# Clears moved beside an expert layer, an opening put in order of use, and three tiles' weights fetched during an attention

## The chip, the core and the metric

The kernel runs on one core of a Trainium2 chip. The metric is the device time in microseconds (us) of one execution; it is shown as the median of a few executions. TensorE (PE) multiplies, VectorE (DVE) and ScalarE (ACT) do elementwise work and reductions, GpSimd (POOL) does elementwise work and starts the gathers and scatters that go by an index, and SyncE (SP) starts most of the plain transfers. Each of these has its own queue of instructions and works through it in order.

## The reference, cut to what matters

Everything is float32. x has 4 batches of 512 rows of 256, and the context has 4 batches of 1601 rows of 256.

```
x = x + L0_xattn(ctx, layernorm(x))   # 8 heads of 128; keys and values from [layernorm(ctx), layernorm(latents)]
x = x + L0_ffn(layernorm(x))          # 8 experts 256->1024->256, top 2, at most 512 rows per expert
x = x + L1_xattn(ctx, layernorm(x))   # 8 heads of 32, keys and values from ctx
x = x + L1_ffn(layernorm(x))          # 8 experts 256->1024->256, top 2, no limit of rows
```

In L0_xattn the latents are normalized again with their own gamma and beta, and the queries attend to 1601 + 512 = 2113 rows.

## The kernel before

The kernel has four stages, one for each line above; they are called A, B, C and D here. A scheduler orders each engine's queue from the program text, except where `in_order` or `keep_in_program_order` fixes it. Buffers come from pools; a load into a buffer waits until the last reader of what lay there is done.

**Opening of A.** SP loads x of batch 0, small vectors, the whole context of batch 0, then `wq`, `wkv`, `wo`, and x of the other batches. DVE takes the moments of all 13 context tiles, then normalizes latents and context. PE turns them (`group`), and `kvin` is written with the columns in an interleaved order: column block b, quarter k, 32 columns. The 512 latents are the first columns of quarter 0. Only when all of `kvin` stands do `queries` and `keys` of head 0 start (L670, L685). PE also works out the product of the values' bias with `wo` (`ps_bo`, L802) here, and POOL adds the output bias to x (L601).

**The clears.** `clear_rows` writes zeros and a mark into two tables in device memory, `rows_a` (2048 rows of 265 numbers) and `rows_b` (18688 rows): 41 transfers on SP, 40 of 530 KB and one of half that, from a zero tile that holds four rows for each partition, so that 4,240 bytes in a row are written. `clear_slots` writes 4 MB of zeros to `slot_x` in 8 transfers, started by POOL. Both stand after the opening and ahead of the first attention step.

**Steps of A.** There are 128 steps n (batch, head, quarter of the queries). A step does `scores` (PE), the maximum `top` (DVE), the exponential `attn` (ACT), `exchange` (16 transfers that swap blocks of 32 partitions, 12 started by SP and 4 by ACT), and in the next step `turn` (DVE) gives `pT`. `weigh` (PE, `ps_o`) follows in steps n + 1 to n + 3. The scores have a single buffer, so the scores of step n + 1 wait for the exponential of step n. The lists `later[n]` put keys of the next head, values, the next batch's context (`load_ctx`, `keys_input`) and the routing of stage B between the pieces.

**B.** Keys and values of L1_xattn for two batches, from `cT`, then 8 experts; SP fetches each expert's weights (2 MB), its rows `sx`, and stores `slot_y`.

**C.** 16 units of 13 steps, with the order of PE, DVE, ACT and POOL written out by hand (`in_order`, L1342). `load_first_weights` (L1279) fetches the first half (1 MB) of expert 0's weights for stage D, in eight pieces of 128 KB, at the start of the last batch.

**D.** Tiles of 256 rows: 8 first tiles, one for each expert, then 13 further tiles and, if there are more, others. `first_tile` loads rows from `rows_a` and weights `w_e` (2 MB) from a pool of four buffers; `further_tile` gathers both by index. For each tile `turned` transposes the rows (PE, L1439), `hidden` is the first product (L1451), and `second` the second (L1470). `told` reads target rows and shares from the rows (DVE, L1401, L1429). During the first tiles `route2` and `table` route the last batch.

## Time and profile before

| | us |
|---|---|
| median of 3 runs (2989.96 to 2995.00) | 2993.43 |
| the profiled execution, its own time | 2993.88 |
| its span, first to last instruction | 2992.2 |

| stretch of the span | PE busy | granted clock | share of DMA |
|---|---|---|---|
| 0 to 45 (opening of A) | 13.84 | 1.00 | 0.75 |
| 45 to 145 (first steps of A) | 70.59 | 0.86 | 0.81 |
| 145 to 1640 (rest of A) | 1480.13 | 1.00 | 0.39 |
| 1640 to 1940 (B) | 284.13 | 0.97 | 0.31 |
| 1940 to 2645 (C) | 613.88 | 0.93 | 0.11 |
| 2645 to 2730 (first tiles of D) | 67.35 | 0.88 | 0.55 |
| 2730 to 2992 (rest of D) | 248.09 | 0.98 | 0.51 |

Each row is one stretch. PE busy is in us and is to be held against the length of the stretch; the clock is the share of full speed that PE was granted; the share of DMA is the mean busy share of the core's 16 DMA engines. In the lists of instructions that follow, a line gives start, duration, engine, line of the code, operation, output and input, and count; a bracket gives the idle time before it and what ended it.

### The profile page before, as it was taken

What the parts mean: (1) busy time and instruction counts of PE and PEld (TensorE: products, weight loads), DVE (VectorE), ACT (ScalarE), POOL (GpSimd) and SP (SyncE); (2) the same over time, 40 slices, a digit from 0 to 9 for tenths busy, and PEclk for the clock granted to TensorE, in tenths of its full rate; (3) what the DMA queues carried; (4) which work ended last, traced back from release to release, by engine and by line L of the source; (5) the groups of instructions that cost most, each with busy time, mean ns of one, the idle gap of its engine ahead of it and who ended that gap; (6) DMA issues with size and microseconds to landing.
All of it is one profiled execution on the core that took longest, in us unless ns stands there. A gap on an engine that the chain in (4) does not pass through costs nothing.

```text
span 2992.2 us, 35534 instructions
## 1 busy us (share of the span) xinstructions
PE 2778.0 (93%) x13426; PEld 1839.3 (61%) x13426; DVE 1456.4 (49%) x2324; ACT 933.3 (31%) x1312; POOL 400.0 (13%) x308
## 2 busy tenths in 40 slices
PE   5699999999999999999997999879989898898998
PEld 2466676667766667666665566634444444466887
DVE  4256447544475444554454200178777768741110
ACT  2133234323343233333331221124434344341221
POOL 1000000100001000000000100022314223333442
PEclk9899999999999999999998899979999999898999
DMA  8743334433344333333334333110101110055552
GB/s 297 236 124 95 98 92 103 117 92 89 95 113 109 90 94 91 99 93 97 95 94 120 117 106 115 47 46 17 28 24 41 29 37 23 11 181 169 185 173 72
DMA packets 165103, 295.95 MB, mean 99 GB/s; under 512 B 43287, under 2 KB 81752, under 8 KB 161848
## 3 DMA queue, kind: packets, MB, share of 16 engines
q1 hardware_dynamic: 124024, 204.45, 24.4%
q0 software_dynamic: 16320, 53.42, 5.9%
q10 hardware_dynamic: 24576, 35.68, 4.6%
q8 instruction: 109, 1.79, 0.3%
q14 instruction: 74, 0.61, 0.1%
HBM read 97.86 MB, written 49.76 MB: 49 GB/s over the span
## 4 chain that ended last, share of the span: by engine, by line
PE 82%; DVE 7%; issue 3%; DMA 3%; ACT 3%; SPq 2%; POOL 1%; POOLq 0%; DVEq 0%; ACTq 0%
PE ps_o L772 15%; PE ps_s L735 15%; PE ps_v L718 7%; PE ps_k L685 7%; PE ps_w L1188 6%; PE ps_y L1470 4%; PE ps_h L1451 4%; PE ps_h L970 4%; PE ps_y L983 4%; DVE tops L1149 2%; PE ps_o L1219 2%; DVE sum L1210 2%; PE ps_p L783 2%; PE ps_v L945 2%; PE ps_q L670 2%
## 5 line engine op out<-in xcount | busy, mean ns | idle before, releaser
L743 DVE TENSOR_REDUCE top<-ps_s 128x1 f32<-128x2113 f32 x128 | 301.8, 2358 | 574.8 <-PE ps_s L735 574.8
L772 PE MATMUL ps_o<-pT,v 128*128 128x256 f32 x2176 | 521.5, 382 | 7.7 <-DVE pT L764 7.7
L735 PE MATMUL ps_s<-kT,qT 128*128 128x512 f32 (+1 forms) x1280 | 488.9, 527 | 26.3 <-ACT attn L749 26.0
L772 PEld LDWEIGHTS ps_o<-pT,v 128*128 128x128 f32 x2176 | 411.4, 191 | 124.8 <-issue 70.3
L735 PEld LDWEIGHTS ps_s<-kT,qT 128*128 128x128 f32 x1280 | 241.8, 191 | 275.7 <-issue 239.9
L749 ACT ACTIVATE attn<-ps_s,top 128x2113 f32<-128x2113 f32 x128 | 259.0, 2024 | 486.5 <-DVE top L743 448.8
L764 DVE STREAM_TRANSPOSE pT<-swapped 128x2176 f32<-128x2176 f32 x128 | 312.4, 2441 | 70.8 <-DMA swapped<-attn 60.3
L1149 DVE TENSOR_REDUCE tops<-ps_s 128x2 f32<-128x1024 f32 (+1 forms) x224 | 237.4, 1104 | 135.2 <-PE ps_s L1138 135.0
L685 PE MATMUL ps_k<-kvin,wkv 128*128 128x512 f32 (+1 forms) x640 | 262.0, 534 | 5.0 <-ACT kT L692 5.0
L1188 PE MATMUL ps_w<-asked,keyed 64*128 64x256 f32 (+1 forms) x1664 | 244.2, 415 | 20.5 <-DVE tops L1149 9.5
L718 PE MATMUL ps_v<-wkv,kvin 128*128 128x256 f32 x1088 | 253.5, 381 | 0.0
L1201 ACT ACTIVATE pT<-ps_w 128x1024 f32<-128x1024 f32 (+1 forms) x176 | 179.5, 1024 | 192.5 <-PE ps_w L1188 190.4
L1188 PEld LDWEIGHTS ps_w<-asked,keyed 64*128 64x128 f32 (+1 forms) x1664 | 147.0, 189 | 143.2 <-ACT pT L1201 60.7
L718 PEld LDWEIGHTS ps_v<-wkv,kvin 128*128 128x128 f32 x1088 | 204.9, 190 | 32.7 <-issue 3.3
L1210 DVE TENSOR_TENSOR sum<-sum,pT 128x1024 f32<-128x1024 f32 (+1 forms) x128 | 181.0, 1414 | 10.7 <-ACT pT L1201 3.9
L692 ACT ACTIVATE kT<-ps_k,bqk 128x512 f32<-128x512 f32 (+1 forms) x160 | 97.3, 621 | 268.7 <-DMA swapped<-attn 129.8
L1210 POOL TENSOR_TENSOR sum<-sum,pT 128x1024 f32<-128x1024 f32 x48 | 124.1, 2585 | 345.7 <-ACT pT L1201 345.5
L685 PEld LDWEIGHTS ps_k<-kvin,wkv 128*128 128x128 f32 x640 | 116.5, 192 | 80.9 <-issue 67.1
L1451 PE MATMUL ps_h<-xT,w_e 128*128 128x256 f32 x640 | 143.9, 383 | 10.2 <-issue 10.2
L1138 PE MATMUL ps_s<-kT,qT 32*128 32x512 f32 (+1 forms) x1024 | 140.5, 577 | 12.5 <-ACT kT L936 6.8
L725 ACT COPY v<-ps_v 128x512 f32<-128x512 f32 x144 | 80.0, 561 | 224.9 <-PE ps_v L718 156.2
L1470 PE MATMUL ps_y<-w_e,hT 128*128 128x256 f32 x640 | 144.4, 385 | 0.0
(261 smaller groups left out, 2615.1 us busy)
## 6 DMA issues: line engine op xcount, KB each, us to landing
swapped<-attn SPq DMA_DIRECT2D x1536, 68.0 KB
swapped<-attn ACTq DMA_DIRECT2D x512, 68.0 KB
rows_b<-empty SPq DMA_DIRECT2D x36, 530.0 KB
w<-in_w_dram SPq DMA_DIRECT2D x16, 1024.0 KB
w_e<-in_wall_dram SPq DMA_DIRECT2D x7, 2052.0 KB
cT<-in_ctxT_dram SPq DMA_DIRECT2D x4, 1601.0 KB
keyed<-kT SPq DMA_DIRECT2D x32, 200.1 KB
ctx_b<-in_ctx_dram SPq DMA_DIRECT2D x4, 1536.0 KB
```

Source lines behind the costliest of these rows:

```text
L685: nc.tensor.matmul(ps[:, :n], lhsT=wkv[:, c, hs], rhs=flat_kvin[c][:, j0 : j0 + n], start=c == 0, stop=c == DC - 1,)
L718: nc.tensor.matmul(ps[:, k, :], lhsT=flat_kvin[c][:, j * P : (j + 1) * P], rhs=wkv[:, c, cols], start=c == 0, stop=c == DC - 1,)
L735: nc.tensor.matmul(flat[:, j0 : j0 + n], lhsT=qT[:, t * P : (t + 1) * P], rhs=kT[:, j0 : j0 + n], start=True, stop=True,)
L743: nc.vector.tensor_reduce(top, flat[:, :L], AX.X, ALU.max, negate=True)
L749: nc.scalar.activation(attn[:, :L], flat[:, :L], AF.Exp, bias=top, accum_out=total)
L764: nc.vector.transpose(pT[:, :, k * P : (k + 1) * P].rearrange("p c (a i) -> p a c i", a=4), swapped.rearrange("p a (c i) -> p a c i", i=32),)
L772: nc.tensor.matmul(ps, lhsT=v[:, j - parts[part][0], (h % 2) * DH0 : (h % 2 + 1) * DH0], rhs=pT[:, j, :], start=j == 0, stop=j == NB - 1,)
L1149: nc.vector.tensor_reduce(tops[u][:, t : t + at // n, 2 * pair : 2 * pair + 2, j0 // 512], of, AX.X, ALU.max,)
L1188: nc.tensor.matmul(ps[:r, s, pair * QH : (pair + 1) * QH], lhsT=keyed[o][64 * s : 64 * s + 64, pair, j * P : j * P + r], rhs=asked[u % 3][ ...
L1210: (nc.gpsimd if k else nc.vector).tensor_tensor(to, to, pT[:r], ALU.add)
L1451: nc.tensor.matmul(ps[:, f, :], lhsT=w(at, P), rhs=xT[:, c, :], start=c == 0, stop=c == DC - 1,)
L1470: nc.tensor.matmul(ps, lhsT=hT[:, f, r * P : (r + 1) * P], rhs=w(WB1 + f * D, D), start=f == 0, stop=f == FC - 1,)
```

## The change

1. `clear_rows` becomes a generator. It is advanced six transfers at a time in the expert loop of B, after the fetch of the next expert's weights. Its source is one row, read four times by a zero stride, so pieces are 1,060 bytes.
2. `clear_slots` is started by SP, one transfer at steps 4, 6, ... 18 of A.
3. The opening loads in order of use: first x and four context tiles, then the latents' vectors, head 0's slices of `wq` and `wkv`, then the rest. The moments go by groups of four tiles, and normalization moves from DVE to ACT. `keys` is cut by quarters, so that `keys(0)` needs the latents alone. The engines' order is fixed.
4. `ps_bo` and the output bias of batch 0 go to step 13 of A.
5. `load_first_weights` fetches the weights of three tiles (6 MB) into memory that C no longer uses; `room(k)` rotates D's weights through four places. The last, conditional tile shares these, where it had a place of its own.
6. Three tiles of integers come from a short-lived pool `brief`; the vectors of A reuse its memory. `counts_i` is made three tiles ahead of the end.

```diff
-    def clear_slots(zeros):
-        for i in range(SLOTS // (4 * P)):
-            nc.gpsimd.dma_start(
-                slot_x[i * 4 * P : (i + 1) * 4 * P, :].rearrange("(p r) d -> p r d", p=P), zeros
+    def clear_slots(zeros, i):
+        tc.keep_in_program_order(
+            nc.sync.dma_start(
+                slot_x[i * 4 * P : (i + 1) * 4 * P, :].rearrange("(p r) d -> p r d", p=P),
+                zeros.unsqueeze(1).to_broadcast([P, 4, D]),
...
+    brief = brief_of.enter_context(tc.tile_pool(name="brief", bufs=1))
+    iota_i = brief.tile([P, NT, E], I32, name="iota_i")
...
-                nc.sync.dma_start(
-                    some.rearrange("(p r) d -> p r d", p=P), empty[:, : some.shape[0] // P, :]
-                )
+                tc.keep_in_program_order(
+                    nc.sync.dma_start(
+                        some.rearrange("(p r) d -> p r d", p=P),
+                        empty.unsqueeze(1).to_broadcast([P, some.shape[0] // P, PAY]),
+                    )
+                )
+                yield
...
+        for n0 in range(0, NM - 1, 4):
+            nc.sync.dma_start(ctx_b[:, n0 : n0 + 4, :], of_ctx[:, n0 : n0 + 4, :])
+            if n0 == 0:
+                load_vectors(gbl, "gamma_lat", "beta_lat")
+                load_vectors(bqk, "bq", "bk", "bv")
+                nc.sync.dma_start(wq[:, :, :DH0], of_wq[:, :, :DH0])
+                nc.sync.dma_start(wkv[:, :, :DH0], of_wkv[:, :, :DH0])
+                load_vectors(gbm, "gamma_media", "beta_media")
...
-            def keys(j0):
-                n = min(512, LP - j0)
+            def keys(k):
+                n = 512 if k < 4 else P
...
-                        rhs=flat_kvin[c][:, j0 : j0 + n],
+                        rhs=kvin[:, c, : NB - 1, k, :] if k < 4 else kvin[:, c, NB - 1, :, :],
...
-        early, late = keys_input(0, ctx_b)
-        for s in early + late:
+        stats, turns = context[::2], context[1::2]
+        for s in (
+            latent[:2] + stats[:1] + latent[2:] + fill[:2] + stats[1:2] + turns[:1] + stats[2:3]
+            + turns[1:2] + fill[2:3] + stats[3:] + turns[2:3] + fill[3:4] + turns[3:] + fill[4:]
+        ):
             s()
-        empty = one.tile([P, 4, PAY], F32, tag="lat", name="empty")
-        clear_rows(empty)
-        clear_slots(empty[:, :, :D])
...
+        for i in range(SLOTS // (4 * P)):
+            later[4 + 2 * i].append(lambda i=i: clear_slots(empty, i))
+        later[13].append(output_bias)
...
             if e + 1 < E:
                 w_next = expert_weights(wexp, "w1", "w2", e + 1)
+                for _ in range(6):
+                    next(clear, None)
...
+            t = kv1.tile([P, KV], F32, tag="kv", name="w_kv")
+            rest = t[:, WIDE:]
+            nc.sync.dma_start(rest[:, : WIDE - WB1], a["wall"][:P, WB1:])
+            nc.sync.dma_start(t[:, :WIDE], a["wall"][P : 2 * P, :])
+            nc.sync.dma_start(cw[:, :WIDE], a["wall"][2 * P : 3 * P, :])
...
+        def room(k):
+            if k % 4 == 2:
+                return cw[:, :WIDE]
+            if k % 4 == 3:
+                return new.tile([P, WIDE], F32, tag="w", name="w_e")
+            return kv1.tile([P, KV], F32, tag="kv", name="w_e")[:, :WIDE]
...
-        more.append(lambda: further_tile(SURE, spare, spare))
+        more.append(lambda: further_tile(SURE, E + SURE, spare))
```

## The prediction

> **What bounds the kernel now.** I read the granted clock first (0.968 over the span), then the busy time by stretches, then the instructions in order of time wherever PE isn't full.
>
> ```profile
> 0.00:45.00 45.00, 13.84 (x54) 8.22 (x55) 25.48 (x130) 6.40 (x13) 11.57 (x28) 1.00 0.75 249
> 45.00:145.00 100.00, 70.59 (x213) 41.40 (x213) 24.11 (x17) 23.66 (x32) 0.09 (x1) 0.86 0.81 282
> 145.00:1640.00 1495.00, 1480.13 (x5540) 1006.22 (x5538) 778.93 (x988) 479.89 (x656) 41.32 (x48) 1.00 0.39 99
> 2645.00:2730.00 85.00, 67.35 (x317) 56.07 (x318) 28.74 (x144) 19.52 (x40) 18.95 (x17) 0.88 0.55 184
> ```
>
> These rows give, for a stretch: its length, busy PE, weight load, DVE, ACT, POOL, the clock, DMA share and GB/s. From 145 to 1640 PE is full. It is not in the first 145 us, nor at the start of D; there lies what a change of order can win.
>
> ```profile
> 43.46 1.96 PE L670 MATMUL ps_q<-kvin,wq 128*128 128x512 f32 x4
> 53.06 3.87 PE L735 MATMUL ps_s<-kT,qT 128*128 128x512 f32 x10 [0.33 <-ACT kT L692]
> 58.53 3.60 PE L685 MATMUL ps_k<-kvin,wkv 128*128 128x512 f32 x8
> 72.55 4.58 PE L685 MATMUL ps_k<-kvin,wkv 128*128 128x512 f32 x8 [5.04 <-ACT kT L692]
> 117.33 5.83 PE L735 MATMUL ps_s<-kT,qT 128*128 128x512 f32 x10 [18.35 <-ACT attn L749]
> 141.80 3.87 PE L735 MATMUL ps_s<-kT,qT 128*128 128x512 f32 x10 [1.09 <-ACT attn L749]
> ...
> 48.79 52.95 SPq L378 DMA_DIRECT2D rows_b<-empty  x30
> 101.84 73.75 SPq L756 DMA_DIRECT2D swapped<-attn  x91
> ...
> 115.16 2.02 ACT L749 ACTIVATE attn<-ps_s,top 128x2113 f32<-128x2113 f32 x1 [19.00 <-DMA swapped<-attn]
> ...
> 2704.88 8.99 PE L1451 MATMUL ps_h<-xT,w_e 128*128 128x256 f32 x32 [9.52 <-issue]
> 2728.93 6.42 PE L1451 MATMUL ps_h<-xT,w_e 128*128 128x256 f32 x29
> ...
> 2703.85 0.15 DVE L1401 CAST to<-rows 128x1 int32<-128x1 f32 x1 [21.81 <-DMA out_dram<-y,to]
> ```
>
> The first queries start at 43.46, the scores of step 0 at 53.06. SP issues clears until 101.74, and only then the first exchange, whose attn had stood since about 61. ACT, stuck in its own four transfers, starts an exponential at 115.16, and PE stood still 18.35 us for it. The scores of step 5 come at 141.80. In D, DVE waits 21.81 us for a tile's rows. The wait is put down to a store of results, but the rows' transfers (issued from 2679 on) are queued behind weights of 2 MB each, at 300 to 430 GB/s. The fifth tile starts at 2728.93.
>
> **The opening.** The instruction list of the changed program shows something that the diff doesn't: the memory of `brief` goes to `gbl` and `bqk`, so SP's third load waits for DVE's copy of `iota_i`, which stands behind the moments of x and a square root. x lands at about 4.0 (376 GB/s between 3 and 4, next to nothing after). With 0.46 us for a pair of moments (12 pairs from 13.69 to 19.25), that copy comes at 7, not 1; the head's weights are issued by 11 and land by 13, still in time for a use at 20.
>
> Now the chain, with durations from the rows of before. Each normalization of the latents is 1.9 moments + 1.5 scale + 1.4 apply, done at 9 and 14. Moments and scale of the first context group end at 18, ACT's four applications and its column write at 20.4. Queries and keys(0) are 3.5, with a cold clock 5: 25.4. DVE then takes qT and the groups in turn, each with a round trip to ACT for the root: scales at 28, 32.5 and 39.7 (the tail's root stands behind kT(1) on ACT). keys(1) end at 37.5, keys(2) at 43, keys(3) and (4) at 46.6. The scores of step 0 end at 50, not 56.9.
>
> For the first steps: top 2.4, exponential 2.0, scores of step 1 at 54.3. In the list, the context load of batch 1 now goes ahead of all exchanges, and DVE's 13 moments of it ahead of the second maximum. It is issued at 43.5, lands by 50, and DVE is through at 60: the second maximum 2 us late. Scores of step 2 start at 64.7, of step 3 at 75.4 (DVE's 13 applications and the first turn lie before), with values between them to 81.6; values and the first weighing, 10.8; step 4 from 92.4 to 96; 6.9 of weighing, queries and keys; step 5 at 103. Against 141.8 that wins 38 to 39; I take 38.
>
> **A rule that speaks against this.** After 5.04 us of idle the 8 matmuls at 72.55 took 4.58, and 3.60 at 58.53: 1.0 lost; after 18.35 us, 2.0. The Trainium skill, TensorE: Matmul & The Clock Gate (Part 1: The HAM clock gate), says that an idle window of some 3.4 us halves PE's clock and that as long a busy time restores it, hence at most 1.7 us for a gap. The new opening cuts PE's work into four bursts with gaps of 3 to 5 us: by the rule up to 6.8, by the rows 2 to 4; the queries at 43.46 even ran at full speed after short gaps. I have put 3.2 into the chain (1.5, 0.8 and some in the transposes); with the rule in full it would be 34 won.
>
> **What A takes on.** `ps_bo`: 8 products are 16 instructions of 0.216 us (6.91 for 32 in a row of D) = 3.5 us, now in PE's full stretch. They were hidden by a PE that waited for DVE. The DVE copies (0.23 each) and the products take turns between keys and scores in the list, so nothing more should stand still: 3.5, bounds 3 and 8.4 (8 times the 1.05 of one turn at 33.66 to 36.71). The clears of `slot_x` move from POOL's queue to SP, each behind its step's 12 exchanges. A step's exchanges already hold SP for 73.75/91 = 0.81 each, 9.7 of a step of 8.8 to 15. One more issue costs 0.5, and 0.52 MB at 345 GB/s (the loads of x at 20 to 27, pieces of 1 KB) 1.5. In the short steps DVE has 1.47 of slack between turn and top (259.83 to 261.30), so most of it is hidden: 1 us in all, bounds 0 and 12. POOL's four bias additions (2.8) are due before a projection two steps on. Net gain of A: 38 - 3.5 - 1 = 33.5.
>
> **B.** The 41 clears write 21.9 MB. The first six stand ahead of the second `cT`, but are issued at about 1648 (POOL's memset is ahead of its scatters in the list) and need 3.26 MB / 345 = 9.4; DMA moves nothing from 1660 to 1670, and `cT` is issued at 1674.97, when PE has let go of its memory. After that, six stand behind each `slot_y`, ahead of the load of `sx` for a tile three experts (86 us) later and of weights that are needed 43 us later. Cost 0, bounds 0 and 9.4; a gain is out, as nothing is removed there.
>
> **C.** 5 MB more in the last batch, 15 us at 345. Behind them on SP are loads of `asked` that are wanted 12 steps, some 40 us, later: 0, bounds 0 and 3.
>
> **D.** Between 2650.9 and 2728.9 PE has four first products with transposes (7.34 each), three second products (6.91) and about 7.5 of routing: 57.6 of 78. So 20.4 is waiting and slow clock. After the change the first three tiles' weights are there; the fourth and fifth (2 MB each, 6 us) have over 30 us; rows no longer stand behind five weights, and the conditional tile's 2 MB leave this stretch. But DVE's list puts the first tile's xT behind the moments of the last batch: its first product starts 4 later; and in the routing chain stands a wait for the fifth tile's rows, 1. Gain 20.4 - 5 = 15, bounds 8 and 19. `counts_i` (0.16 on DVE) moves to three tiles ahead of the end and is read only behind the last tile, as before: 0, with 40 us of cover.
>
> **Sum.** 33.5 + 0 + 0 + 15 = 48.5. 2993.9 - 48.5 = 2945.4 in the profiled execution's own time, which lies 0.45 above the median: 2945.
>
> **The rivals.**
> - *The first steps take back what the opening wins.* DVE and ACT, in order, hold steps 1 and 2 until batch 1's context has landed and is normalized. For it: the list. Against it: the loads ahead (7.4 MB) are through by about 30. With the context at 65 A wins 19 instead of 33.5: 2959.
> - *D stays bound by something else*: the eight scatters of rows to `rows_b` follow one another at 2.6 to 7 us each on POOL, ahead of the adds. If PE ends up waiting for them, D wins 4: 2956.
> - *The opening is better than my chain*: short gaps keep the clock up and DVE overlaps more; step 5 at 95: 2937.
> - *Slower: the clears make B bound by DMA.* The Trainium skill, DMA: Bandwidth & Descriptors (Measured), wants transfers of 1 MiB for 75% of peak; these have half that, in pieces of 1,060 bytes. Other transfers in the 300 us of B are 31 MB, 89 us at 345. The clears have 211 us, so they need 104 GB/s; under 84 they eat all 48.5 us, and at 60 the time is about 3099. 1 KB pieces ran at 345 to 351 here, and 4,240-byte ones at 395 to 399: by rule and rows alike a mere 63 to 80 us of DMA.
> - The change not doing what it says is excluded by the lists: the clears are gone from the opening.
>
> **How the numbers follow.** Chances: my sum 0.58 (2938 to 2953), the held first steps 0.15, D bound elsewhere 0.12, the better opening 0.11, slower 0.04. The range 2930 to 2961 leaves out the ends of these. 0.2% (6 us) is about what can be told from no change: faster 0.95, same 0.01, slower 0.04.
>
> **What would show it.** First queries at about 20, scores of step 5 near 103, no SP row of clears before B but eight single ones in A; 1640 to 1940 as long as before with DMA at 0.5; D's fifth tile 15 us earlier against the end of C. I'm wrong if PE shows idle before `ps_h` in B, if a wait on batch 1's context lasts over 10 us on DVE, or if the fifth tile starts less than 8 us earlier.

## The result, and the profile after

| | before | after |
|---|---|---|
| median of 4 runs each, us | 2994.22 (2989.96 to 2997.24) | 2965.70 (2964.83 to 2966.69) |
| profiled execution, its own time | 2993.88 | 2966.02 |
| its span | 2992.2 | 2964.2 |
| mean granted clock | 0.968 | 0.967 |

The ratio is 0.9897 (95% interval 0.9885 to 0.9909): 28 us are gone, where 48.5 had been forecast, and the time lies outside the range of 2930 to 2961. Cut at the same instructions in both profiled executions, the span divides so:

| part | cut at | forecast | measured |
|---|---|---|---|
| A | last `ps_p` of A | 33.5 | 34.4 |
| B, with keys and values of C | last `ps_p` of A to first `ps_q` of C | 0 | −2.7 |
| C | first `ps_q` to last `ps_n` | 0 | −6.2 |
| D, up to POOL's last scatter of results | | 15 | 5.7 |
| end, behind that scatter | | not forecast | −3.2 |

Here is PE by stretches in the profile after (columns as in the prediction: length, PE, weight load, DVE, ACT, POOL, clock, DMA share, GB/s):

```profile
0.00:20.00 20.00, 2.43 (x9) 1.73 (x10) 14.01 (x83) 3.08 (x7) 2.00 (x15) 1.00 0.58 166
20.00:108.00 88.00, 78.09 (x245) 44.64 (x246) 48.25 (x125) 39.09 (x61) 0.00 (x0) 0.94 0.47 135
108.00:1606.00 1498.00, 1482.85 (x5553) 1008.34 (x5551) 767.99 (x937) 476.52 (x652) 44.77 (x54) 1.00 0.40 100
2622.00:2700.00 78.00, 65.92 (x319) 55.67 (x308) 26.85 (x141) 19.96 (x40) 18.58 (x17) 0.87 0.46 142
```

PE has its first queries at 20 instead of 43, and from 20 to 108 it is busy for 78 of 88 us. From 108 to 1606 it is full, as it was. The last row, the start of D, is what disappoints: 12 us of it are still idle, and the clock of 0.87 is no better than before.

Now the instructions in order of time, PE first and then SP's queue:

```profile
19.77 3.91 PE L725 MATMUL ps_q<-kvin,wq 128*128 128x512 f32 x4 [3.52 <-DVE kvin L666]
47.53 2.91 PE L792 MATMUL ps_s<-kT,qT 128*128 128x512 f32 x8
65.11 5.57 PE L792 MATMUL ps_s<-kT,qT 128*128 128x512 f32 x10 [2.04 <-ACT attn L806]
104.24 3.77 PE L792 MATMUL ps_s<-kT,qT 128*128 128x512 f32 x10
...
55.01 54.50 SPq L813 DMA_DIRECT2D swapped<-attn  x60
109.61 0.61 SPq L183 DMA_DIRECT2D slot_x<-scrap  x1
```

Queries of head 0 start at 19.77 (before: 43.46), scores of step 0 end at 50.44 (56.93), scores of step 5 start at 104.24 (141.80). The exchanges now begin at 55.01, with no clears in front, and one clear of `slot_x` stands behind the exchanges of a step.

And the start of D, PE, DVE and POOL of the same execution:

```profile
2621.61 1.07 PE L1316 MATMUL ps_n<-sum,ones 128*32 128x256 f32 x16 [3.04 <-DVE sum L1288]
2631.68 9.54 PE L1546 MATMUL ps_h<-xT,w_g 128*128 128x256 f32 x32 [0.94 <-DVE xT L1535]
2675.81 7.07 PE L1546 MATMUL ps_h<-xT,w_e 128*128 128x256 f32 x32
2690.19 0.61 PE L1605 MATMUL ps_x<-over,ones 128*128 128x16 f32 x2 [5.56 <-DVE xT L1535]
2698.68 7.07 PE L1546 MATMUL ps_h<-xT,w_e 128*128 128x256 f32 x32
...
2689.33 0.21 DVE L1490 CAST to<-rows 128x1 int32<-128x1 f32 x2 [12.58 <-DMA out_dram<-y,to]
...
2685.55 1.56 POOL L1578 DMA_INDIRECT out_dram<-y,to  x1 [7.08 <-DMA out_dram<-y,to]
```

From the last `ps_n` of C to the first product of D there are 10.07 us; before there were 3.81. And DVE still waits 12.58 us ahead of a cast that makes `to`, with a store to `out_dram` as the releaser. For comparison, this is the same place in the kernel before (PE, DVE, POOL, SP), and then three more lines of the profile after (DVE, POOL, SP):

```profile
2719.55 0.61 PE L1510 MATMUL ps_x<-over,ones 128*128 128x16 f32 x2 [3.93 <-DVE xT L1440]
...
2704.10 0.68 DVE L1440 COPY xT<-tp 128x512 f32<-128x512 f32 x1
2718.68 0.21 DVE L1401 CAST to<-rows 128x1 int32<-128x1 f32 x2 [12.87 <-DMA out_dram<-y,to]
...
2694.22 1.56 POOL L1483 DMA_INDIRECT out_dram<-y,to  x1 [1.29 <-DMA out_dram<-y,to]
...
2657.53 0.67 SPq L1425 DMA_DIRECT2D w_e<-in_wall_dram  x1
2695.43 0.33 SPq L1425 DMA_DIRECT2D w_e<-in_wall_dram  x1
```

```profile
2671.29 0.21 DVE L1490 CAST to<-rows 128x1 int32<-128x1 f32 x2 [8.80 <-DMA out_dram<-y,to]
...
2667.52 1.56 POOL L1578 DMA_INDIRECT out_dram<-y,to  x1 [1.62 <-DMA out_dram<-y,to]
...
2643.87 0.42 SPq L1519 DMA_DIRECT2D w_e<-in_wall_dram  x1
```

Before, DVE stood twice behind such a store. The wait of 21.81 us ended with the cast at 2703.85; `xT` of the fourth tile follows at 2704.10, and that tile's first product at 2704.88. So the 9.52 us for which PE stood there ended with `xT`, and `xT` stood behind the cast; the fourth tile's weights had been issued at 2657.53. The second wait, 12.87 us ahead of the fifth tile's `xT`, cost PE 3.93 us. After the change the first wait is 8.80 us and costs PE nothing, and the second is 12.58 and costs PE 5.56. Weights are not late here either: SP issued the fifth tile's at 2643.87, and its first product starts at 2698.68.

### The profile page after: what moved, and what is told of

It is laid out like the page before. It is cut to its first block, busy times and chain, and to the rows that moved or that the text cites. A ratio compares the mean times of both kernels' runs of the same rounds, so it can differ in the third digit from the quotient of the medians.

```text
span 2964.2 us, 35563 instructions
## 1 busy us (share of the span) xinstructions
PE 2782.5 (94%) x13426; PEld 1841.3 (62%) x13426; DVE 1458.7 (49%) x2333; ACT 942.5 (32%) x1330; POOL 391.9 (13%) x301
## 5 line engine op out<-in xcount | busy, mean ns | idle before, releaser
L821 DVE STREAM_TRANSPOSE pT<-swapped 128x2176 f32<-128x2176 f32 x128 | 312.4, 2441 | 34.4 <-DMA swapped<-attn 24.2
L1266 PE MATMUL ps_w<-asked,keyed 64*128 64x256 f32 (+1 forms) x1664 | 246.6, 418 | 20.2 <-DVE tops L1227 9.5
L1279 ACT ACTIVATE pT<-ps_w 128x1024 f32<-128x1024 f32 (+1 forms) x176 | 179.5, 1024 | 195.2 <-PE ps_w L1266 191.5
L1216 PE MATMUL ps_s<-kv,qT 32*128 32x512 f32 (+1 forms) x1024 | 143.4, 594 | 12.2 <-ACT kv L1007 6.5
L1054 PE MATMUL ps_y<-w,hT 128*128 128x256 f32 x512 | 112.8, 379 | 0.0
L1041 PE MATMUL ps_h<-sxT,w 128*128 128x512 f32 x256 | 111.8, 594 | 0.5 <-issue 0.4
```

The source lines that it names most:

```text
L821: nc.vector.transpose(pT[:, :, k * P : (k + 1) * P].rearrange("p c (a i) -> p a c i", a=4), swapped.rearrange("p a (c i) -> p a c i", i=32),)
L1216: nc.tensor.matmul(pss[i // 2][:, i % 2, at : at + n], lhsT=qTs[b][rows, o, q0 : q0 + P], rhs=kvs[b][0][o][rows, j0 : j0 + n], start=True, ...
L1266: nc.tensor.matmul(ps[:r, s, pair * QH : (pair + 1) * QH], lhsT=keyed[o][64 * s : 64 * s + 64, pair, j * P : j * P + r], rhs=asked[u % 3][ ...
L1279: nc.scalar.activation(pT[:r], ps[:r], AF.Exp)
```

## The experiments

Each ran beside the kernel before on the same chip. Where a row says "C to tile 4", it is from the last `ps_n` of C to the first product of D's fifth tile: 81.83 us before, 77.07 after. Within one kernel the time falls by some 1.6 us for each 0.001 of mean granted clock (95 runs of the changed kernel and those below, each against the mean of its own kernel; correlation −0.80), and the medians of the kernel before were 2994.2 to 2997.5 on the chips used. So medians differ by a few us with nothing changed, and what follows rests on the rows of the traces. The changed kernel itself has a median of 2966.2 over its 8 runs; "under the changed kernel" is against that.

**The scatters of C earlier.** Theory: the first rows of D wait for the scatters of rows, which are late.

```diff
-                spread(s0 + 10, route2(b - 1, one, ps_s, "s"), 2, 24)
+                spread(s0 + (8 if b == B - 1 else 10), route2(b - 1, one, ps_s, "s"), 2, 24)
```

> The changed kernel, but in the last batch of C the routing of the batch before it (and with it the 16 scatters of rows) starts two steps earlier, at s0 + 8 in place of s0 + 10. Theory: in the changed kernel the buffers of D lie over the memory of C, so the rows of the first tile cannot be loaded, and the moments of the last batch not be taken, before the last scatter of C has read its rows (issued at 2624.28, landed about 2627.2). Two steps are some 6.5 us, so the scatters end by the time that C itself ends: the first product of D's first tile starts about 5 us instead of 10.07 after C's last ps_n, and the time falls by 4 to 6 us, to about 2960. Rival: the first tile is late because of DVE's order alone (moments and closing ahead of its xT); then the gap stays at 8 or more and the time within 1 us of 2965.7. The instructions up to the middle of the last batch are those of the changed kernel: this is also a second profile of A, B and most of C. If the granted clock in C is a matter of where idle gaps fall against a fixed beat, its slow stretches come again at the same gaps.

2968.34 (ratio 0.991, 0.9892 to 0.9928), so nothing was won; from the last `ps_n` to the first `ps_h` 8.86 instead of 10.07. DVE and SP of this run there:

```profile
2629.30 0.42 DVE L1347 TENSOR_TENSOR x<-x,got 128x256 f32<-128x256 f32 x1
...
2629.85 4.25 SPq L1511 DMA_DIRECT2D rows<-rows_a  x8
```

The loads of rows are issued 0.13 us behind the end of C's last addition on DVE, not behind the scatters. In the program the first load of rows waits for every engine's last use of C's memory. Before, `kvst.close()` stood ahead of D's pools and gave D the memory of keys and projections, which C had left; then that load waited for the scatters to `rows_a` alone. The changed kernel keeps those tiles for weights, so D's rows lie over memory that C uses to the end.

**A fourth buffer for rows.** Theory: the fifth tile's rows wait for a free buffer. Rival: for `to`, behind a store.

```diff
-        three = st.enter_context(tc.tile_pool(name="d_three", bufs=3))
+        three = st.enter_context(tc.tile_pool(name="d_three", bufs=4))
```

> The changed kernel with four buffers for the rows of a tile in D instead of three. Theory: the stall ahead of tile 4 (5.56 us idle at 2690.19 and 2 us of slow clock behind it) comes from DVE's order: the target rows of tile 7 are read ahead of the turned rows of tile 4, and the load of tile 7's rows waits for the buffer that PE's transposes of tile 4 free at 2683.24, and takes 6 us. With a fourth buffer that load waits for tile 3 only; the stall goes and the time falls by 6 to 7.5 us, to about 2959. Rival: the stall is due to the stores of results (the profile names out_dram as the releaser) or to the queue of weights; then it stays at 5 us or moves to the next tile, and the time stays within 1.5 us of 2965.7.

2966.31 (0.9903, 0.9888 to 0.9918). SP and DVE of this run:

```profile
2658.34 12.00 SPq L1511 DMA_DIRECT2D rows<-rows_a  x3
...
2689.75 0.21 DVE L1490 CAST to<-rows 128x1 int32<-128x1 f32 x2 [12.46 <-DMA out_dram<-y,to]
```

All rows are issued by 2670.34, and yet the cast runs at 2689.75 behind a wait of 12.46. Rows are not what it waits for: the rival holds. Both edits together:

> Both edits: scatters of the last batch of C two steps earlier and four buffers for rows in D. If the two waits are separate, the gains add: 10 to 13 us off the changed kernel, 2953 to 2956. If one wait takes the place of the other, the gain is that of the larger alone, 2958 to 2960.

2968.10 (0.9911, 0.9896 to 0.9926): nothing.

**D undone.** The changed kernel up to B, with C's and D's weights, pools and `kvst.close()` as before. (The changed kernel holds `cT` and the projections of C in one tile, `cw`; here they have tiles of their own again.)

```diff
-    cw = w1p.tile([P, DC * (M + 3 * D)], F32, name="cw")
...
+        cT = w1p.tile([P, DC, M], F32, tag="cT", name="cT")
...
-            nc.sync.dma_start(t[:, :WIDE], a["wall"][P : 2 * P, :])
-            nc.sync.dma_start(cw[:, :WIDE], a["wall"][2 * P : 3 * P, :])
...
+        four = st.enter_context(tc.tile_pool(name="d_four", bufs=4))
```

> The changed kernel with the part on D's weights undone: only the half of the first tile's weights is fetched in C, keys and values have memory of their own that is given back ahead of D, and D has four buffers for weights. Opening, clears, short-lived integers and moved bias stay as changed. Theory: D gained little (its tile 3 stall of 9.5 us and slow clock gone, 6.3 us lost at its first tile), so the time is 3 to 5 us above the changed kernel, 2968.5 to 2971, except for what the granted clock in C does. Rival 1, my prediction's own account: D gained 15, so the time is 2980. Rival 2: the prefetch of 5 MB is what slows C by 5.8 us; then C is as short as in the kernel before (C's first to last ps_n 604.1 instead of 606.6), and the time is 2966 or less.

2969.81 (0.9921, 0.9907 to 0.9936). So part 5 of the change is worth about 3.6 us net, not 15. The stall ahead of the fourth tile is back: from the third tile's first product to the fourth's there are 23.64 us (before 23.94, after 14.25). So part 5 is what took it away. The way may lead through the store: from its start on POOL to DVE's cast there are 9.63 us before, with 2 MB of weights issued 1.2 us behind it (2695.43), and 3.77 after, where SP issues no weights from 2643.87 to 2676.04. That link is not tested. Two lengths of this run bear on later questions: B up to the first expert took 71.67 (after: 74.83), C 690.62 (after: 694.73).

**More buffers for target rows.** Theory: `to` and `share` have five buffers each; the seventh tile's `to` needs a buffer that the scatter-add of an earlier tile still reads, and that add is the one at 2685.55 on POOL. DVE, in order, holds the fifth tile's xT behind that cast.

```diff
+        ten = st.enter_context(tc.tile_pool(name="d_ten", bufs=10))
...
-            to = five.tile([P, GR], I32, tag="to", name="to")
-            share = five.tile([P, GR], F32, tag="share", name="share")
+            to = ten.tile([P, GR], I32, tag="to", name="to")
+            share = ten.tile([P, GR], F32, tag="share", name="share")
```

> The changed kernel with a pool of ten buffers, in place of five, for the two small tiles of a D tile (target rows and shares). The four buffers for rows left the stall ahead of tile 4 as it was: DVE's read of the target rows came at 2689.75 although the rows were there by about 2673. Theory: the profile's releaser is right. The target rows of tile 7 reuse the buffer of tile 2, which the second add of tile 2's results to out_dram reads; POOL issues that add at 2685.55, behind eight scatters to rows_b and four earlier adds, and it lands some 3.5 us later. With ten buffers the read waits for nothing, the idle 5.5 us and the 2 us of slow clock behind it go: tile 4's first product starts 15 us after tile 3's instead of 22.9, and the time falls by 6 to 8 us against 2965.7 to 2966.3, to about 2959. Rival: DVE waits for POOL elsewhere too (the y tiles, also five); then the stall moves to the next tile and at most 2 us are won.

2957.84 (0.9866, 0.9848 to 0.9884): 8.3 under the changed kernel. PE of this run:

```profile
2675.46 7.07 PE L1547 MATMUL ps_h<-xT,w_e 128*128 128x256 f32 x32
2684.11 0.29 PE L1606 MATMUL ps_x<-over,ones 128*128 128x16 f32 x2
2690.38 7.07 PE L1547 MATMUL ps_h<-xT,w_e 128*128 128x256 f32 x32
```

Fourth to fifth tile is 14.92 now, 22.87 after the change and 24.05 before it. `ps_x` (0.61 at the cold clock behind the wait) takes 0.29 with no wait. That is the second of the two stalls that the prediction had laid to weights in front of rows. The first, ahead of the fourth tile in the kernel before, has the same releaser, but more buffers alone were not tried there.

**The first tile's memory.** The rows of the first two tiles and xT of the first lie in the memory of C's projection weights; the third tile's weights are not fetched during C.

```diff
-            nc.sync.dma_start(cw[:, :WIDE], a["wall"][2 * P : 3 * P, :])
...
-                got = three.tile([P, PAY], F32, tag=f"rows{r}", name=f"rows{r}")
+                if e < 2:
+                    at = (GR * e + r) * PAY
+                    got = cw[:, at : at + PAY]
+                else:
+                    got = three.tile([P, PAY], F32, tag=f"rows{r}", name=f"rows{r}")
```

> The changed kernel with the rows of D's first two tiles and the turned rows of the first in the memory that held C's projections, which is free in the last batch; the third tile's weights, that lay there, are fetched at the start of D instead, and the two places change their turns. Theory: the late first product (10.07 us behind C's last ps_n, 3.81 in the kernel before) comes from memory: D's tiles lie over C's, so that the rows wait for the last reader of all of C, its last addition to x on DVE (with the scatters two steps earlier SP issued the loads at 2629.85, right behind that addition at 2629.30 + 0.42). With memory of their own the rows are there early and the first product starts about 4 after C's last ps_n: 5 to 6 us off, to about 2960. Rival: the 6 us come back at tile 2, whose 2 MB of weights are then fetched at D's start together with those of tiles 3 and 4 (7 us each at 300 GB/s); then tile 2 starts as late as before and the time stays within 2 us of 2966.

2961.52 (0.9881, 0.9865 to 0.9896). PE of this run:

```profile
2620.25 1.07 PE L1316 MATMUL ps_n<-sum,ones 128*32 128x256 f32 x16 [3.02 <-DVE sum L1288]
2623.19 7.96 PE L1552 MATMUL ps_h<-cw,w_g 128*128 128x256 f32 x24
2667.49 7.07 PE L1552 MATMUL ps_h<-xT,cw 128*128 128x256 f32 x32
2694.26 5.99 PE L1552 MATMUL ps_h<-xT,w_e 128*128 128x256 f32 x27
```

The first product follows the last `ps_n` by 2.94 us instead of 10.07, so it was the memory. C takes 694.72, no less for the 2 MB that it no longer fetches. But fourth to fifth tile is 26.77 instead of 22.87: the fifth tile waits for the chain of stores, not for its own start, and 4 of the 7 us are given back there. With both edits:

> Both edits of D: the first tile's rows in memory of their own, and ten buffers for target rows and shares. If they are separate waits, 11 to 14 us off the changed kernel in the stretch from C's last ps_n to D's fifth tile (77 us there, 63 to 66 here), and 2952 to 2955 in all. If POOL's chain of scatters and adds bounds this stretch, the second adds nothing to the first: 2959 to 2961.

2950.61 (0.9858, 0.984 to 0.9876), 15.6 under the changed kernel; C to tile 4 takes 61.67. Against the 81.83 of before that is 20.2 us. From the first tile's first product to the fifth's there are 58.88, where before there were 78.02.

**Idle products in the gaps of C.** In C the profile after shows no more work than before, yet 6.2 us more. This kernel puts products of the identity, whose results nothing uses, where PE waits: in five units (9, 6, 5, 5 and 6 of them) and ahead of two small products of the routing.

```diff
+    def busy(ps, n):
+        for _ in range(n):
+            nc.tensor.matmul(
+                ps, lhsT=ident, rhs=ident.unsqueeze(1).to_broadcast([P, 4, P]), start=True, stop=True
+            )
...
+            busy(ps.rearrange("p a q -> p (a q)"), {1: 9, 3: 6, 7: 5, 11: 5, 13: 6}.get(u, 0))
```

> The changed kernel with idle products on PE (ident times ident, 128x512, about 0.36 us each, into a buffer that the next instruction overwrites anyway) in C just where PE waited 2.8 to 4.4 us: ahead of the turned maxima of units 1, 3, 7, 11 and 13 (9, 6, 5, 5 and 6 of them), and ahead of two small products of the routing in batches 1 to 3 (5 each). They compute nothing that is used. Theory: the slow clock in C is caused by these gaps, each of which costs 1.7 us or a multiple of it; with them filled the granted clock stays up behind them. Eight such slow stretches of the changed kernel's profile, worth 16 us, lie behind filled gaps; the idle products may run into the waits' ends here and there, 1 to 3 us: C is 10 to 15 us shorter, and the time is about 2953. Rival: the slow stretches come from something other than idling (heat, load, a fixed beat); then C keeps 45 us of slow clock and the time is 2966 to 2970.

2961.96 (0.9877, 0.986 to 0.9895). All of C in the kernel before, after the change, and in this one:

```profile
1958.53:2647.10 688.57, 611.74 (x5091) 319.33 (x5091) 513.98 (x776) 283.67 (x338) 208.50 (x118) 0.94 0.10 28
```

```profile
1926.88:2621.61 694.73, 617.01 (x5090) 322.05 (x5090) 514.43 (x775) 283.69 (x338) 205.98 (x119) 0.93 0.12 34
```

```profile
1926.22:2620.91 694.69, 647.75 (x5202) 333.26 (x5202) 514.26 (x775) 283.70 (x338) 210.86 (x119) 0.96 0.11 34
```

The clock rises from 0.93 to 0.96; what PE loses to the slow clock, worked out as busy time by one less the clock in stretches of 1 us, falls from 45.7 to 27.3. So the gaps make the slow clock. The length of C stays, where 10 to 15 us less had been expected: the added products hold up some units by as much as the others gain.

**The clears of B later.** No clears in the round of the first expert, seven in the others.

```diff
-                for _ in range(6):
+                for _ in range(7 if e else 0):
```

> The changed kernel with the row clears in B begun one expert later: none beside the first keys and values, seven at a time behind the fetches from the third expert's weights on. In the changed kernel and its variants B took 73.5 to 74.8 us from A's last product to the first expert, 71.8 in the kernel before. Theory: the six clears beside the load of cT cost 0.4 to 0.8 us of waiting for cT and nothing else; without them the first ps_k has no wait for cT, its granted clock may fall as before or not, and B's stretch is 72 to 74: in time not more than 1 us off. Rival 1: the clears cost the whole 3 us, and the stretch is 71.8 again. Rival 2: seven clears at a time in the later experts delay sx or weights; then ps_h waits in the experts, which it does not in the changed kernel.

2964.35 (0.9885, 0.9866 to 0.9904). The first `ps_k` no longer waits for `cT`, and yet B up to the first expert takes 73.71 (71.76 before, 74.83 after): a wait of 0.84 us for `cT` is gone and the rest of the 3 is not. Nor does that wait go with the clears: the two kernels of the next experiment have none in B, and one of them waits 0.64 us there.

**The clears of rows back in the opening.** The changed kernel with all 41 ahead of the first exchange, in its own pieces of 1,060 bytes.

```diff
+            for _ in clear_rows(marked):
+                pass
...
-                for _ in range(6):
-                    next(clear, None)
```

> The changed kernel with the 41 row clears back behind the opening and ahead of the first exchange (from one row, so in pieces of 1,060 bytes); none in B. Everything else as changed: opening in order of use, slot clears one by one, D with the weights fetched early. Theory: most of A's 37.6 us come from the exchanges that no longer stand behind the clears, only 6.5 from the opening's order. The scores of step 0 still end at about 50.4; SP then issues clears from 44 to about 100 (21.9 MB at 345 to 400 GB/s), the scores of step 5 come at 130 to 140 in place of 104.24, and the time is 26 to 36 us above the changed kernel: 2992 to 3002. Rival: the opening's order carries the gain (exchanges would hide behind clears that share the DMA engines); then step 5 comes before 120 and the time is under 2982.

3036.11 (1.0121, 1.0104 to 1.0139): 34 us above the end of what was expected. B up to the first expert takes 74.64, though no clears are left in it. The same from a tile that holds four rows for each partition, as before, so that 4,240 bytes in a row are written:

```diff
-                        empty.unsqueeze(1).to_broadcast([P, some.shape[0] // P, PAY]),
+                        empty[:, : some.shape[0] // P, :],
...
+        marked = one.tile([P, 4, PAY], F32, tag="lat", name="marked")
```

> The changed kernel with the 41 row clears back ahead of the first exchange, as in e10, but from the zero tile of four rows of the kernel before, so in pieces of 4,240 bytes. Theory: e10 was 69 us slower than the changed kernel, not 26 to 36, because pieces of 1,060 bytes moved 216 GB/s where pieces of 4,240 bytes moved 378 to 397 in the kernel before: 101 us of clears for 55. With large pieces the clears end near 95, the scores of step 5 come at 130 to 137, and the time is 26 to 32 us above the changed kernel, 2993 to 2999, 37 to 43 below e10. Rival: the loads and not the pieces made e10 slow (clears issued from 34 on, against the weights of the opening); then the time stays above 3020.

2993.28 (0.9989, 0.9982 to 0.9996; 22 runs). The stretch in which the clears run, from the one and then the other (columns as above), and third a stretch of B in the profile after, beside clears and an expert's weights:

```profile
95.00:115.00 20.00, 0.00 (x0) 0.00 (x0) 0.00 (x0) 0.00 (x0) 0.00 (x0) 0.50 1.11 215
```

```profile
75.00:95.00 20.00, 11.03 (x43) 7.71 (x41) 0.00 (x0) 3.09 (x6) 0.00 (x0) 0.89 1.01 385
```

```profile
1720.00:1748.00 28.00, 28.00 (x104) 18.69 (x102) 2.25 (x5) 4.91 (x9) 0.00 (x0) 1.00 0.95 226
```

Each time the DMA engines are full, but the short pieces go at 215 GB/s and the long ones at 385. It isn't shortness alone, nor that one row is read four times: a clear of `slot_x` in the profile after writes pieces of 1,024 bytes, read four times from one row too, and moved at 316.

```profile
110.87:112.53 1.66, 1.66 (x7) 1.16 (x7) 0.32 (x1) 1.66 (x3) 0.00 (x0) 1.00 0.93 316
```

By the trace a piece of 1,024 bytes took 48 ns of a DMA engine there, and one of 1,060 took 85 in the stretch of B above and 87 in that from 95 to 115. What it is about 1,060 is open; the clear of `slot_x` is also short, 0.5 MB, and stands alone. With the long pieces the clears in the opening cost what had been reckoned: step 5 comes at 131.36, the whole opening without the moved clears wins 5.5 us of A (the 3.5 of `ps_bo` taken off), and the median is 2.2 under that of before. B up to the first expert takes 73.57, again without clears. The third row shows B near the limit of DMA while PE is still full.

**The clears moved alone.** Before, with parts 1 and 2 of the change.

```diff
-        clear_rows(empty)
-        clear_slots(empty[:, :, :D])
...
+            later[4 + 2 * i].append(lambda i=i: clear_slots(empty, i))
...
+                for _ in range(6):
+                    next(clear, None)
```

> The kernel before with one part of the change alone: the row clears moved beside the expert layer (from one row), the slot clears started by SP at steps 4 to 18. Opening, keys, product of the values' bias, memory of the integers, C and D as in the kernel before. Theory: the exchanges no longer stand behind the clears, the opening is 6.5 us later than in the changed kernel, and the bias product costs nothing in A: the scores of step 5 end near 111, A ends 30 to 31 earlier than in the kernel before (34.4 in the changed one), C and D as before; 2964 to 2968, no slower than the whole change by more than 3. Rival: DVE and ACT are still held in steps 1 and 2 by the context of batch 1, which is loaded ahead of the exchanges; then A wins 20 or less and the time is over 2974. The stretch behind POOL's last scatter (8.9 us in the kernel before, 11.8 to 12.8 in all others) tells whether its 3 us come with the clears' part (12 again) or with the opening's (8.9).

2972.68 (0.9923, 0.9907 to 0.9939): some 23 of the 29 us come from this alone. A wins 32.35 (step 5 at 109.19), and the end behind POOL's last scatter is 12.39 instead of 8.91: those 3.5 us come with the clears' part. B up to the first expert takes 71.84, and C 689.95. So with the clears in B, but `cT` and the projections in tiles of their own, neither stretch is longer by more than 1.4.

**The changed kernel again.**

> The changed kernel itself, once more, for its spread and its profile beside the others of this chip. Theory: its time moves by some 6 us from run to run with the mean granted clock (about 2.9 us for each 0.001), as e7 did (0.972: 2949.1, 0.968: 2959.9), so the lengths of A, B and C differ between two profiles of one kernel: C is 694.7 in the first one, and anything from 690 to 701 here; D's stretch from C's last ps_n to its fifth tile is within 1 us of 77.07. Rival: the slow clock falls in the same places each time; then every stretch is as in the first profile to 0.5 us.

2967.00 (0.9894, 0.9876 to 0.9911). C takes 694.88, unit by unit as in the first profile to about 0.3 us, so the rival holds there: it is no chance of one execution. Beside it ran the version with both edits of D and the later clears:

> The changed kernel with three edits: rows of D's first tiles in memory of their own, ten buffers for target rows and shares, and the row clears begun one expert later. Theory: the two edits of D won 15 us (2950.6 in e7), the later clears win at most 1: 2948 to 2952. Rival: if the clears cost 3 us in B, 2946 to 2948.

2953.95 (0.9852, 0.9835 to 0.9869), 2 us above what was expected and no better than without the later clears. But its C takes 690.94, with the text of C that gives 694.74 without the later clears. The first unit of C in the kernel before, after the change, and in this one:

```profile
1958.53:2043.02 84.49, 74.02 (x513) 34.23 (x516) 63.49 (x65) 25.76 (x29) 18.53 (x12) 0.86 0.09 24
```

```profile
1926.88:2015.04 88.16, 77.75 (x512) 36.48 (x516) 63.47 (x65) 25.76 (x29) 18.47 (x12) 0.81 0.09 23
```

```profile
1927.69:2012.29 84.60, 74.15 (x514) 34.24 (x518) 63.49 (x65) 25.77 (x29) 18.49 (x12) 0.86 0.09 24
```

DVE, ACT and POOL do the same work in the same time; PE is busy 3.6 us longer because the clock is 0.81 instead of 0.86, and the unit is 3.56 us longer.

The traces' record of the granted clock shows what goes with it. In each of the 17 profiles the clock changes only on one beat of 3.41 us. Where that beat falls against the first `ps_q` of C can be told from the start of the first slow stretch behind it:

| first slow stretch starts, us behind the first `ps_q` | profiles | first unit of C, us |
|---|---|---|
| 9.18 to 9.52 | 3: before, D undone, this one | 84.3 to 84.6 |
| 9.57 to 10.04 | 11: after, the changed kernel again, nine more | 87.9 to 88.3; 89.35 with the idle products |
| 10.50 and 11.10 | 2: ten buffers for target rows, the later clears | 86.3 and 86.7 |
| 18.82 | 1: the clears moved alone | 83.6 |

Between 9.52 and 9.57 the unit grows by 3.3 us, as a third slow stretch, of 10.24 us, comes in at about 30. The eleventh unit does the same. There PE has a gap of 2.77 to 2.79 us ahead of `ps_r`. In twelve profiles it begins 1.36 to 1.48 us behind a beat, and the unit takes 40.55 to 40.84 us. In four (before, this one, ten buffers, the later clears) it begins 1.54 to 2.30 behind a beat, and the unit takes 38.0. (With the idle products this gap is filled.) Kernels with the merged `cw` stand on both sides each time. So the lengths of these units go with the beat; no run set it on purpose, and edits ahead of C moved it.

**The clears of `slot_x` started by POOL.** The version with both edits of D, and in `clear_slots`

```diff
-            nc.sync.dma_start(
+            nc.gpsimd.dma_start(
```

> The two edits of D (e7), and the slot clears started by POOL again in place of SP. Theory: the 3 us behind POOL's last scatter (8.9 in the kernel before, 11.8 to 12.8 in every other kernel) come with the part that e13 and e14 alone have in common, the slot clears on SP; with POOL starting them the stretch is 8.9 again. POOL has nothing else to do in the first steps and starts five of the clears at once, 2.6 MB beside the first exchanges, which costs 0 to 4 us there. Time 2947 to 2952. Rival: the stretch stays at 12 or more, and its cause is another; then 2950 to 2955.

2949.71 (0.984, 0.9826 to 0.9853), the best version found, though its interval overlaps that of the same kernel with the clears on SP. POOL's last scatter of results before, after, and in this one:

```profile
2981.74 1.55 POOL L1483 DMA_INDIRECT out_dram<-y,to  x1 [3.02 <-DMA out_dram<-y,to]
```

```profile
2950.57 1.56 POOL L1578 DMA_INDIRECT out_dram<-y,to  x1 [2.97 <-DMA out_dram<-y,to]
```

```profile
2938.26 1.54 POOL L1585 DMA_INDIRECT out_dram<-y,to  x1 [3.40 <-DMA out_dram<-y,to]
```

Against the spans of 2992.2, 2964.2 and 2949.4 the ends of these leave 8.91, 12.07 and 9.60 us (8.9 had been expected for the last). In every kernel with these clears on SP it is 11.8 to 12.8. So the 3 us go with the queue that starts the clears, some 2,600 us earlier; by what means is open.

## Why the prediction was right or wrong

**Right: A.** Forecast 33.5, measured 34.4. The chain of the opening held nearly row by row: queries at 20, scores of step 0 done at 50, step 5 at 103 were forecast; 19.77, 50.44 and 104.24 came. PE's cold bursts were rightly weighed by the rows: the rule of one full slow window for each gap would have made the win 34 at step 5, and it was 37.6. `ps_bo` was forecast at 3.5: the gain over before stands at 37.7 just ahead of step 13 and at 34.2 from there on. The clears of `slot_x` cost nothing that shows in the steps (forecast 1). The rivals of held first steps and of a better opening are out. Most of the win is the exchanges that no longer stand behind the clears: those moved alone won 32.35 of it.

**Wrong: D, "20.4 is waiting and slow clock", less 5.** This is the step that failed, and in it the wait: "rows no longer stand behind five weights". The 20.4 was nearly right as what could be won, since with two more edits the stretch from the first tile to the fifth falls from 78.0 to 58.9, by 19.1; but the change doesn't remove its causes. The row of DVE named the releaser, a store to `out_dram`, and the prediction set that aside for weights in front of rows. A fourth buffer of rows moved the rows and left the stall; ten buffers for `to` and `share` removed it, and brought fourth to fifth tile from 22.87 to 14.92. Of the two stalls that the store made before, the change took the first, 9.52 us of PE ahead of the fourth tile (from the first tile's first product to the fourth's there are 44.13 instead of 53.97). A likely reason is that no weights then move beside the store, but that was not tested. Of the second it took 1.2. The second term, "its first product starts 4 later", was 6.26: the first rows wait for the end of C, because D's rows lie over C's memory. So D gained 5.7 instead of 15. The rival "D stays bound by something else", D wins 4, came nearest, and its mechanism was POOL's chain: scatters to `rows_b`, and behind them the adds to `out_dram`, which are what DVE waited for.

**Wrong: C at 0 with a bound of 3.** It lost 6.2, and 5.3 of that is PE busy for longer with the same instructions (611.74 and 617.01). The transfers, which the prediction weighed, are not what it lost by: 3.7 lie in the first unit, ahead of them, and C is 694.72 and 694.74 in two versions that fetch 2 MB less in it. 2.6 lie in the eleventh unit. Both go with the place of C's products against the beat of the clock. Of 14 versions with the merged `cw` eleven stand on the long side of the first unit and three do not, and the three kernels with separate tiles have a short one; in the eleventh unit separate tiles stand on both sides. So the merging may move the place of C against the beat, but is not enough to lengthen a unit. The prediction had no term for the beat.

**Wrong: B at 0.** It lost 3.1 up to the first expert and won 0.35 behind it. The clears are not the cause: with clears and separate tiles it is 71.7 and 71.8 (the change with D undone, the clears alone), and in kernels with `cw` 73.5 to 74.8, with clears in B or without any (74.64 and 73.57). From the first `ps_k` to the first expert, before and after:

```profile
1650.80:1706.91 56.11, 49.60 (x181) 32.90 (x182) 16.25 (x55) 8.42 (x17) 7.77 (x8) 0.91 0.25 82
```

```profile
1617.40:1675.61 58.21, 51.47 (x181) 33.39 (x181) 15.75 (x52) 8.31 (x17) 7.84 (x8) 0.90 0.47 130
```

PE is busy 1.9 us longer with the same number of products, and waits 0.84 for `cT`. Up to the first expert the slow stretches last 20.5 us together in the three kernels with separate tiles and 23.9, one beat more, in all with `cw`. So it goes with the merging in part 5. Which wait of PE brings the extra beat was not isolated. The first clears came when they were forecast: 1648 by the clock of the kernel before is 1614 here, and SP issued the first six between 1607.75 and 1625.

**The slower rival** did not happen, but its price was off. It was reckoned with 345 GB/s, from loads with pieces of 1,024 bytes; the clears, in pieces of 1,060, ran at 215 to 226, so 21.9 MB take 101 us and not 63. (The 4,240-byte pieces, put at 395 to 399, ran at 377 from 60 to 75 and at 397 from 95 to 101.) With the 89 of other transfers that is 190 of 300 us. PE waits for nothing in the experts of B, so the forecast of no loss there was right with less room than thought.

**Not seen at all: the end**, 3.2 us. The move of `clear_slots` from POOL to SP was costed for its place in SP's queue, where it is free, and not for what it does to the end.

The sum of the errors: D 9.3, C 6.2, the end 3.2, B 2.7, less 0.9 that A won more, is 20.5, and 48.5 less that is the 28.0 measured.

## What to carry to other kernels

When a wait's releaser is named in the trace, follow that one first: here it was right, and a plausible transfer that was queued at the same time was not; a small buffer whose reader is a slow store can hold an engine as surely as a large one. When memory is given to early loads, ask which tiles move into memory that is still in use, since that is a new wait at the seam of two stages. Time a clear or a store by the very same pieces in the same direction, not by a load of about that length. And when a stage full of short waits gets a few us longer with nothing changed in it, hold its start against the beat of the granted clock before a cause is looked for in its text.

## What the runs showed of the hardware

Writes from on-chip memory to device memory in pieces of 1,060 bytes, read four times from one row, ran at 215 GB/s with the DMA engines full; from four rows in a row, 4,240 bytes, at 385, and the same opening was 41 us faster by it, each against the kernel before on its own chip. Pieces of 1,024 bytes, read four times from one row, moved at 316 in a clear of 0.5 MB.

In each of the 17 profiles the granted clock is 1.00 or 0.50 and changes only on one beat of 3.41 us. That quantum agrees with the window of 3.4 us at half speed that the Trainium skill, TensorE: Matmul & The Clock Gate (Part 1: The HAM clock gate), describes. But a gap of PE of 2.8 us was long enough in twelve profiles, where it began at most 1.48 us behind a beat, so that at least 1.93 us of the beat were idle; where it began 1.54 or more behind, with 1.87 idle or less, it brought no slow clock in four. In C the slow clock took 46 of 695 us.

The time between POOL's last scatter and the end of the span was 8.9 or 9.6 us where POOL started the clears of `slot_x`, and 11.8 to 12.8 where SP did.
